# Moving the exponentials, coefficients, powers and K of heads 16 to 31 to later groups of a state-space and FFN kernel

## The chip, the cores and the metric

The kernel runs on one core of one Trainium2 chip. The metric is the device time of one execution in microseconds (us); lower is better. The kernel before takes 305.06 us, the median of three runs (304.72 to 305.21).

## The reference

The input x has 128 sequences (b), 32 heads (h) and 512 positions (l). Each head first gets a causal convolution with a kernel K that is made from 64 complex exponentials, plus a skip term; positions beyond a sequence's length are zeroed. Then comes a gated FFN over the 512 positions with 1376 inner features, its inputs rounded to fp8, and the result is added to x:

```
dt = exp(log_dt);  A = -exp(log_A_real) + 1j*A_imag;  dtA = A*dt
Ct = C * (exp(dtA) - 1) / A
K[h, l] = 2 * Re( sum_n Ct[h, n] * exp(dtA[h, n] * l) )
y = causal_conv(x, K) + x * D;   y[b, :, l >= length[b]] = 0
q = fp8(y)
hidden = silu(q @ gate.T) * (q @ up.T)
out = x + fp8(hidden) @ down.T
```

## The kernel before, in words

**Groups.** The 32 heads are worked in eight groups of four, numbered 0 to 7 (loop at line 764). A group has three stages. Gate and up (`gate_up`, line 630) runs over eleven chunks of 128 inner features: TensorE makes `gp` and `up` (line 646, four matmuls each), ScalarE takes silu of `gp` (L654), VectorE multiplies it with `up` (L656), and the product is rounded to fp8 by ScalarE (L621) and VectorE (L622, L623, L624) into `hq`. Then the convolution of the *next* group's four heads runs (`conv`, line 572): per head a matmul `sp` (L490) and five matmuls `cp` (L495 to L499) with a Toeplitz tile `st`; ScalarE copies `sp` to `shared` (L493); VectorE makes `q` and masks it (L576, L586); `sort` (line 589) permutes q by matmuls `pq` (L593), and ScalarE writes `qs` (L601), which the next group's gate and up reads. Between these stand the down matmuls `dp` (L688) of the present group, whose results VectorE adds to x (`put_out`, L701) before they are stored.

**K.** The heads fall into three batches for making K: heads 0 to 3, 4 to 15 and 16 to 31, in the objects `first`, `others[0]` and `others[1]` of class `Powers`. One batch takes these steps: `angles` (VectorE, L254, L52, L54, L264), `magnitudes` (ScalarE, one Exp per head, L269, then an activation at L198 that brings the Silu table back), `sines` (ScalarE, L276, L277, L281), `coefficients` (twelve small VectorE operations, L291 to L304), `products` (six VectorE operations, L309 to L324) and `response` (line 326). `response` makes K by one small matmul for each head into the PSUM tile `kp` and one more for the skip term (L329, L330), copies it to `kt` (VectorE, L333), and writes that to a DRAM buffer `kpad` (L334). `toeplitz` (line 470) reads each head's tile `st` back from `kpad` by two DMAs (L475, L476); there are four `st` buffers. Heads 16 to 19, the first that need batch `others[1]`, are group 4, and their convolution runs in the loop's iteration g = 3.

**Where batch `others[1]` is made before.** Its sixteen exponentials stand ahead of group 0, together with the twelve of `others[0]` (lines 713 to 716). Its angles are spread over the four `put_out` calls of iteration 0, its sines follow at that iteration's end (L827), coefficients and products are spread over the `put_out` calls of iteration 1, five at a time, and `response` is called after the gate and up of group 2 (line 769).

**Other ScalarE work.** `check_q` (line 603) sums the absolute values of q in two halves (L607). `low_halves` (line 535) sums the low halves of the weights (L542), four pieces in each iteration until nineteen are done.

**What sets the order.** Each engine runs its own instructions strictly in the order in which they stand; the build places them there, and `with after(x)` asks that an instruction stand behind x. Data dependencies are kept by semaphores on which an engine waits in place. SP's queue issues the `st`, `x` and `kpad` DMAs one behind the other; group 1's `st` loads and the second batch's `kpad` go through GpSimd's queue.

```
                if g == 2:
                    others[1].response()
...
                some = {0: (others[1].angles(), 2), 1: (itertools.chain(others[1].coefficients(), others[1].products()), 5)}
...
                with after(sent):
                    list(itertools.islice(lows, 4))
```

Of the kernel before, what the change touches and what calls it, by code (L numbers as in the profile page):

```python
# [15 lines left out]
AF = mybir.ActivationFunctionType  # L16
# [41 lines left out]
def ssm_fp8_ffn(  # L58
# [55 lines left out]
    def load_x(g, queue=nc.sync):  # L114
        xg = xp.tile([P, LC, T], F32, name="xg", bufs=1)
        queue.dma_start(
            xg.rearrange("p c (h b) -> p c h b", b=B),
            xT[:, g * HG : (g + 1) * HG, :].rearrange("(c p) h b -> p c h b", p=P),
        )
        return xg  # L120
# [13 lines left out]
    def load_gate_up(w, src, i0, i1, queue=nc.sync):  # L134
        return queue.dma_start(w[:, :, i0:i1], src[:, i0:i1].rearrange("(c p) i -> p c i", p=P))
# [24 lines left out]
    NK = NC + NB  # L160
# [35 lines left out]
    def table(func, ready):  # L196

        return nc.scalar.activation(spare, ready, func)  # L198

    def after(done):  # L200

        return tc.issue_after(done.ins)
# [35 lines left out]
    class Powers:  # L238
# [24 lines left out]
            for o, r in ((self.cos, self.sin), (self.zb[0:N], self.zb[0:N])):  # L263
                yield nc.vector.scalar_tensor_tensor(o, r, -1.0, r, ALU.mult, ALU.min)  # L264

        def magnitudes(self, then=True):
            self.mag = self.tile("mag", NK, shared=False)
            for h in range(self.h0, self.h1):
                done = nc.scalar.activation(  # L269
                    self.mag[:, h - self.h0, :], idx, AF.Exp, scale=wre[:, h : h + 1]  # L270
                )
            with after(done):
                return table(AF.Silu, self.mag[:, 0, 0:1]) if then else done

        def sines(self, between=lambda: None):
            nc.scalar.activation(self.sin, self.sin, AF.Sin)  # L276
# [63 lines left out]
    with after(exp_there), after(square_there):  # L340
        silu_there = first.magnitudes()
# [18 lines left out]
    done, copied, _ = first.response()  # L360
# [32 lines left out]
    shared = [const.tile([P, 2, P], F32, name=f"shared{n}") for n in range(HG)]  # L393
# [170 lines left out]
    def narrow():  # L564
        with ExitStack() as arm:
# [6 lines left out]
            def conv(g, q, j, xg, xs, before):  # L572

                st, loaded = toeplitz(stp, g * HG + j, nc.gpsimd if g == 1 else nc.sync)
                cp, t, convolved, copied = convolve(st, xg, xs, j, inv[:, 0:1], before)
                nc.vector.scalar_tensor_tensor(  # L576
                    q[:, j, :].rearrange("p (k c l) -> p k c l", k=2, c=2),
                    cp.rearrange("p (k c) l -> p k c l", k=2),
                    inv[:, 0:1],
                    t,  # L580
                    ALU.mult,
                    ALU.add,
                    saturate=False,
                )
                words = q.bitcast(I32)[:, j, :]
                made = nc.vector.tensor_tensor(words, words, mask.bitcast(I32), ALU.bitwise_and)  # L586
                return convolved, made, loaded, copied

            def sort(q, qs, j, before):

                pq = ps.tile([P, NQ], F32, name="pq", tag="up")
                for c in range(LC):
                    done = nc.tensor.matmul(  # L593
                        pq[:, OFF[c] : OFF[c] + CAPS[c]],
                        q[:, j, CHUNKS.index(c) * P : (CHUNKS.index(c) + 1) * P],
                        perm[:, 0 : CAPS[c]],
                        start=True,
                        stop=True,
                    )
                with after(before):  # L600
                    return done, nc.scalar.activation(qs[:, j, :], pq, AF.Copy, saturate=False)  # L601

            def check_q(g, q):

                for n in range(2):
                    junk = vp.tile([P, T], F32, name="s")
                    done = nc.scalar.activation(  # L607
                        junk.bitcast(BF16),
                        q[:, n * HG // 2 : (n + 1) * HG // 2, :].rearrange("p h l -> p (h l)"),
                        AF.Abs,  # L610
                        accum_out=fin[:, 2 * g + n : 2 * g + n + 1],
                    )
                return done
# [96 lines left out]
            others = [Powers(n) for n in range(1, len(batches))]  # L710
            with after(copied):
                list(others[0].angles())
            with after(first_sines):
                silu_there = others[0].magnitudes(False)
            with after(silu_there):
                silu_there = others[1].magnitudes()
            with after(silu_there):
                sines_there = others[0].sines()
            list(others[0].coefficients())
            xg, xs = x0, xs0  # L720
            q = yp.tile([P, HG, L], F8, name="q")
            qs = yp.tile([P, HG, NQ], F8, name="qs")
            for j in range(HG):
                convolved, made, loaded, sines_there = conv(0, q, j, xg, xs, sines_there)
                if j == 0:
                    with after(made):
                        list(others[0].products())
                else:
                    with after(convolved):
                        done, sines_there = sort(q, qs, j - 1, sines_there)  # L730
            with after(loaded):
                load_gate_up(uw, upT, 0, I1)
                load_gate_up(gw, gateT, I2, IH)
                load_gate_up(uw, upT, I1, IH)
                load_gate_up(gw, gateT, IH, I)
                loaded = load_gate_up(uw, upT, IH, I)
# [10 lines left out]
            lows = low_halves(vp)  # L747
# [15 lines left out]
            halves = [*whole[:-1], (HG - 1, 0, L // 2), (HG - 1, L // 2, L)]  # L763
            for g in range(G):
                hq, multiplied, done, jobs = gate_up(g, qs, first_loads if g == 0 else {})
                if g == 0:
                    xn_next, xs_next = loads
                xn = xn_next
                if g == 2:
                    others[1].response()  # L770
                if g == G - 1:
                    break
                some = {0: (others[1].angles(), 2), 1: (itertools.chain(others[1].coefficients(), others[1].products()), 5)}
                d = Down(g, hq, xn, whole, ["dp", "dp", "cp", "cp"], *some.get(g, ()))
                xg, xs = x_next, xs_next
                q_done, q = q, yp.tile([P, HG, L], F8, name="q")
                qs = yp.tile([P, HG, NQ], F8, name="qs")

                last, sent = multiplied, None
                for j in range(HG):
                    if j in (0, 2):
                        with after(done):
                            *_, done = jobs.pop(0)
                    with after(last), after(done):
                        last, done, loaded, sent = conv(g + 1, q, j, xg, xs, sent)
                    if j == 1:
                        for n in range(2):  # L790
                            with after(last):
                                last = d.multiply(n, 0, EARLY)
                    if j >= 2:
                        with after(last):
                            last, sent = sort(q, qs, j - 2, sent)
                with after(loaded):
                    if g + 2 < G:
                        x_next = load_x(g + 2)
                if g + 2 < G:
                    xs_next, summed = load_sums(g + 2)  # L800
                with after(summed):
                    xn_next = load_sorted(g + 1)
                with after(sent):
                    list(itertools.islice(lows, 4))
                for n in range(2):
                    with after(last):
                        last = d.multiply(n, EARLY, LATE)
                for n in range(2, HG):
                    with after(last):
                        last, sent = sort(q, qs, n, sent)  # L810
                with after(sent):
                    check_q(g, q_done)
                for job in jobs:
                    with after(done):
                        *_, done = job
                with after(last):
                    last = d.multiply(2, 0, LATE)
                for n in range(HG):
                    if (g, n) == (G - 2, HG - 1):
                        break  # L820
                    with after(last):
                        last = d.multiply(n, LATE if n < 3 else 0, IC)
                    with after(done):
                        done = d.put_out(n)
                if g == 0:
                    with after(sent):
                        others[1].sines()  # L827
# [9 lines left out]
            with after(done):  # L837
                done = before.put_out(HG - 1)
# [135 lines left out]
```

## Time and profile before

| what | value |
|---|---|
| median of three runs | 305.06 us (304.72 to 305.21) |
| the profiled execution's own time | 305.09 us |
| its span in the profile | 303.2 us |
| TensorE's mean granted clock | 0.986 |
| VectorE busy | 264.3 us (87%) |
| ScalarE busy | 181.0 us (60%) |
| GpSimd busy | 50.8 us (17%) |
| the 28 exponentials of L269 ahead of group 0, first start to last end | 10.38 to 16.82 us |
| first gate matmul of group 0 | 28.69 us |

The profile is one execution. PE is TensorE's matmuls and PEld its weight loads, DVE is VectorE, ACT ScalarE, POOL GpSimd, and SPq the queue of SyncE that issues DMAs. A row of the timeline gives the start, the time until the end of the last of the merged instructions, the engine, the line of the kernel, the operation with output and input tiles, and in brackets how long the engine had been idle just before and what released it. Each fp32 matmul appears twice in the counts (x2). The page's first part gives busy times by engine; its second cuts the span into 40 slices of 7.58 us, each digit a tenth of busy time.

### The profile page before, as it was taken

Reading aid. Unit: us, or ns where it says so; the run is one execution under the profiler, and the core shown is the slowest. Engines: PE = TensorE matmul, PEld = TensorE weight load, DVE = VectorE, ACT = ScalarE, POOL = GpSimd, SP = SyncE. Lnnn points to the kernel's source line nnn. Section 1 sums busy time; section 2 is a strip of 40 time slices with the busy share of each in tenths; the row PEclk is TensorE's granted clock in tenths of the full one; section 3 lists DMA queues with packets and bytes.
Section 4 is the critical chain, followed back from the end, with each engine's and each line's share of the span. In section 5 each row is a group of like instructions: output and inputs, shape, how many; then the busy total and the mean of one; then the engine's idle time right before and its main releaser. Section 6 shows DMA issues by size and latency. Waiting matters only on the chain.

```text
span 303.2 us, 4843 instructions
## 1 busy us (share of the span) xinstructions
PE 283.9 (94%) x1708; PEld 171.3 (57%) x1708; DVE 264.3 (87%) x466; ACT 181.0 (60%) x385; POOL 50.8 (17%) x104
## 2 busy tenths in 40 slices
PE   8889999997999999999999999999999999999850
PEld 3467567454774557645774567555774567455330
DVE  5875999989999999969997899969996999899960
ACT  4964783877729783658726782748533881579200
POOL 5771340210002100130002100310003200000030
PEclk9999999999999999999999999999999999999995
DMA  2599999981069602792059404890259430000052
GB/s 83 192 261 381 378 361 341 256 278 44 20 128 243 271 1 50 193 316 111 22 129 311 201 1 89 248 304 21 58 148 294 175 125 0 0 1 3 0 214 72
DMA packets 26039, 47.95 MB, mean 158 GB/s; under 512 B 2848, under 2 KB 15404, under 8 KB 24088
## 3 DMA queue, kind: packets, MB, share of 16 engines
q1 hardware_dynamic: 21784, 26.28, 28.9%
q0 software_dynamic: 4224, 21.29, 20.8%
q8 instruction: 15, 0.25, 0.3%
q14 instruction: 16, 0.13, 0.2%
HBM read 39.03 MB, written 8.54 MB: 157 GB/s over the span
## 4 chain that ended last, share of the span: by engine, by line
DVE 44%; PE 29%; issue 12%; ACT 8%; DMA 3%; SPq 1%; POOL 1%; POOLq 0%; ACTq 0%
PE dp L688 11%; DVE v L656 10%; DVE v L622 10%; DVE hq L623 9%; PE gp L646 5%; DVE q L576 5%; ACT s L654 5%; PE up L646 4%; DVE hq L624 4%; ACT m L621 2%; DMA st<-kpad 2%; PE cp L497 1%; PE cp L495 1%; PE cp L496 1%; DVE q L586 1%
## 5 line engine op out<-in xcount | busy, mean ns | idle before, releaser
L688 PE MATMUL dp<-dw,hq 128*128 128x512 bf16 (+1 forms) x363 | 84.6, 380 | 3.1 <-DVE hq L624 2.5
L654 ACT ACTIVATE s<-gp,psc 128x512 f32<-128x512 f32 x88 | 58.5, 680 | 30.7 <-PE gp L646 30.3
L646 PE MATMUL up<-qs,uw 128*128 128x512 fp8e4 (+1 forms) x352 | 70.3, 321 | 2.3 <-DVE v L656 1.8
L656 DVE SCALAR_TENSOR_TENSOR v<-up,psc,s 128x512 f32<-128x512 f32 x88 | 64.3, 745 | 7.7 <-ACT s L654 7.7
L646 PE MATMUL gp<-qs,gw 128*128 128x512 fp8e4 (+1 forms) x352 | 70.4, 321 | 0.6 <-ACT qs L601 0.6
L688 PEld LDWEIGHTS <-hq 128*128 128x128 bf16 x363 | 33.2, 96 | 44.5 <-DVE hq L624 7.5
L623 DVE SCALAR_TENSOR_TENSOR hq<-m,v 128x1024 bf16<-128x1024 bf16 (+1 forms) x56 | 55.5, 991 | 1.1
L622 DVE SCALAR_TENSOR_TENSOR v<-m,v 128x1024 f32<-128x1024 bf16 (+1 forms) x56 | 55.4, 989 | 1.2 <-ACT m L621 1.2
L621 ACT ACTIVATE m<-v 128x1024 bf16<-128x1024 f32 (+1 forms) x56 | 48.7, 870 | 8.9 <-DVE v L656 8.9
L646 PEld LDWEIGHTS <-uw 128*128 128x128 bf16 x352 | 32.0, 97 | 28.9 <-issue 3.8
L646 PEld LDWEIGHTS <-gw 128*128 128x128 bf16 x352 | 31.9, 97 | 26.4 <-issue 0.7
L601 ACT ACTIVATE qs<-pq 128x376 fp8e4<-128x376 f32 x32 | 14.6, 480 | 30.3 <-PE pq L593 30.3
L701 DVE SCALAR_TENSOR_TENSOR xn<-dp,nsc,xn 128x512 f32<-128x512 f32 (+1 forms) x33 | 23.0, 729 | 9.0 <-PE dp L688 8.8
L493 ACT ACTIVATE shared<-sp,inv 128x128 f32<-128x128 f32 x32 | 11.3, 360 | 27.6 <-PE sp L490 27.6
L576 DVE SCALAR_TENSOR_TENSOR q<-cp,inv,shared 128x512 fp8e4<-128x512 f32 x32 | 23.8, 744 | 2.1 <-PE cp L499 1.5
L111 POOL DMA_DIRECT2D xs<-xT x6 | 3.5, 586 | 116.4 <-PE sp L490 116.4
L706 POOL DMA_INDIRECT out<-xn,index x9 | 9.5, 1060 | 76.8 <-DVE xn L701 72.4
L624 DVE TENSOR_SCALAR hq<-hq 128x1024 bf16<-128x1024 bf16 (+1 forms) x56 | 20.9, 373 | 1.4
L495 PE MATMUL cp<-st,xg 128*128 128x256 f32 x64 | 19.2, 381 | 0.0
L497 PE MATMUL cp<-st,xg 128*128 128x256 f32 x64 | 19.1, 380 | 0.0
L496 PE MATMUL cp<-st,xg 128*128 128x256 f32 x64 | 19.0, 379 | 0.0
L607 ACT ACTIVATE s<-q 128x1024 bf16<-128x1024 fp8e4 x16 | 16.7, 1054 | 0.0
(159 smaller groups left out, 283.7 us busy)
## 6 DMA issues: line engine op xcount, KB each, us to landing
xg<-xT SPq DMA_DIRECT2D x8, 1024.0 KB, 7.7
st<-kpad SPq DMA_DIRECT2D x28, 192.0 KB, 3.8
st<-kpad SPq DMA_DIRECT2D x28, 128.0 KB, 3.5
xs<-xT POOLq DMA_DIRECT2D x12, 256.0 KB, 4.6
dw<-downT SPq DMA_DIRECT2D x2, 1280.0 KB, 19.3
gw<-gateT SPq DMA_DIRECT2D x2, 768.0 KB, 8.6
gw<-gateT SPq DMA_DIRECT2D x1, 1216.0 KB
uw<-upT SPq DMA_DIRECT2D x1, 1216.0 KB
```

The source lines that it names most:

```text
L495: nc.tensor.matmul(cp[:, 1:4:2, :], xg[:, 0, b], st[:, 2:4, :], start=True, stop=False)
L497: nc.tensor.matmul(cp[:, 1:3, :], xg[:, 1, b], st[:, 3:5, :], start=False, stop=False)
L576: nc.vector.scalar_tensor_tensor(q[:, j, :].rearrange("p (k c l) -> p k c l", k=2, c=2), cp.rearrange("p (k c) l -> p k c l", k=2), inv[:, ...
L621: nc.scalar.activation(m, v, AF.Abs, scale=2.0**20 * (1.0 + 2.0**-6), accum_out=acc)
L622: yield nc.vector.scalar_tensor_tensor(v, m, 1.5 * 2.0**14, v, ALU.max, ALU.add)
L623: yield nc.vector.scalar_tensor_tensor(out, m, 1.5 * 2.0**14, v, ALU.max, ALU.subtract)
L624: yield nc.vector.tensor_scalar(out, out, FP8_MAX, -FP8_MAX, ALU.min, ALU.max)
L646: multiplied = nc.tensor.matmul(o[:, :, 0 : CAPS[c]], w[:, c, i * P : (i + 1) * P], qs[:, :, OFF[c] : OFF[c] + CAPS[c]], start=(c == 0), s ...
L654: gated = nc.scalar.activation(s, gp, AF.Silu, scale=pgate)
L656: done = nc.vector.scalar_tensor_tensor(v[:, (i - i0) * T : (i - i0 + 1) * T], up, pup, s, ALU.mult, ALU.mult)
L688: done = nc.tensor.matmul(self.dps[n], self.hq[:, i, j * B : (j + 1) * B], dm[:, i, l0:l1], start=(i == 0), stop=(i == IC - 1),)
L701: added = nc.vector.scalar_tensor_tensor(o, self.dps[n], ndown, o, ALU.mult, ALU.add)
```

## The change

Five things are changed, all to do with batch `others[1]` (heads 16 to 31):

1. Its sixteen exponentials leave the stretch ahead of group 0 and stand in iteration 0, behind the ScalarE copy of the second sorted head; `magnitudes` always ends with the activation that brings the Silu table back. `mag` becomes a tile that both later batches share.
2. In iteration 0 they stand where four `low_halves` were; those of all later iterations move on by one iteration.
3. `check_q` of group 0 is split: its first half stands ahead of group 0 (behind the third head), its second in the convolution stage of iteration 0.
4. The coefficients stay in iteration 1 (three for each `put_out`), and the products move to iteration 2 (two for each `put_out`).
5. `response` is called after the gate and up of group 3 instead of group 2.

```diff
-        def magnitudes(self, then=True):
-            self.mag = self.tile("mag", NK, shared=False)
+        def magnitudes(self):
+            self.mag = self.tile("mag", NK)
...
-                return table(AF.Silu, self.mag[:, 0, 0:1]) if then else done
+                return table(AF.Silu, self.mag[:, 0, 0:1])
...
-                silu_there = others[0].magnitudes(False)
-            with after(silu_there):
-                silu_there = others[1].magnitudes()
+                silu_there = others[0].magnitudes()
...
+                    if j == 2:
+                        with after(sines_there):
+                            sines_there = check_q(0, q, (0,))
...
-                if g == 2:
+                if g == 3:
                     others[1].response()
...
-                some = {0: (others[1].angles(), 2), 1: (itertools.chain(others[1].coefficients(), others[1].products()), 5)}
+                some = {0: (others[1].angles(), 2), 1: (others[1].coefficients(), 3), 2: (others[1].products(), 2)}
...
+                        if g == 0:
+                            with after(sent):
+                                sent = check_q(0, q_done, (1,))
...
                 with after(sent):
-                    list(itertools.islice(lows, 4))
+                    if g == 0:
+                        sent = others[1].magnitudes()
+                    else:
+                        list(itertools.islice(lows, 4))
...
-                with after(sent):
-                    check_q(g, q_done)
+                if g:
+                    with after(sent):
+                        check_q(g, q_done)
```

In the built program the engines' orders differ as follows. On TensorE ahead of group 0, before: `sp`, `cp` of head 0, `sp`, `cp` of head 1, `sp` of head 2, `sp` of head 3, three `cp` of head 2, `pq` of head 0, and so on; after: `sp`, `cp`, `sp`, `cp`, `pq` of head 0, `sp`, `cp` of head 2, `pq` of head 1, `sp`, `cp` of head 3, `pq` of head 2. The 17 `kp` matmuls of the last batch stand before in four pieces (2, 7, 1 and 7) among group 2's last gate and up matmuls; after, in one piece behind the last `up` matmul of group 3 and directly ahead of the `sp` of head 16. The copy to `kt` stands behind the same L624 of VectorE in both, one group later. On SP's queue the write of `kpad` and the `st` loads of heads 16 to 19 follow it, behind the load of group 4's x. ScalarE has two more loads of a function table, around the sixteen exponentials.

More of the change, by code (lines that the diff above doesn't have):

```diff
@@ L601, in sort, with check_q @@
                     return done, nc.scalar.activation(qs[:, j, :], pq, AF.Copy, saturate=False)
-            def check_q(g, q):
-                for n in range(2):
+            def check_q(g, q, halves=(0, 1)):
+                for n in halves:
                     junk = vp.tile([P, T], F32, name="s")
```

## The prediction

> **What bounds the kernel now.** I read the page's slices first: TensorE is full nearly everywhere, and in most slices VectorE is as full.
>
> ```profile
> span 303.2 us, 4843 instructions
> PE 283.9 (94%) x1708; PEld 171.3 (57%) x1708; DVE 264.3 (87%) x466; ACT 181.0 (60%) x385; POOL 50.8 (17%) x104
> PE   8889999997999999999999999999999999999850
> DVE  5875999989999999969997899969996999899960
> ACT  4964783877729783658726782748533881579200
> ```
>
> Then busy times from one first gate matmul to the next, for groups 1, 2, 3 and 4 (us; busy PE, PEld, DVE, ACT, POOL; clock).
>
> ```profile
> 62.48:98.21 35.73, 33.74 (x197) 20.35 (x196) 33.57 (x60) 24.86 (x49) 4.27 (x4) 1.00 0.47 137
> 98.21:133.00 34.79, 34.79 (x232) 21.58 (x231) 32.48 (x53) 21.73 (x47) 3.56 (x4) 1.00 0.51 147
> 133.00:166.30 33.30, 33.09 (x198) 20.21 (x196) 29.84 (x44) 20.62 (x45) 3.56 (x4) 1.00 0.51 163
> 166.30:199.60 33.30, 33.09 (x198) 20.22 (x197) 29.83 (x44) 20.02 (x43) 3.58 (x4) 1.00 0.50 143
> ```
>
> A plain group takes 33.30 us with TensorE busy for 33.09: TensorE's in-order stream is the bound, and VectorE (29.84) follows closely. So only what removes or adds time in that stream moves the end. Three places differ from plain: the stretch ahead of group 0 (28.69 us), group 1 (+2.43) and group 2 (+1.49). The timeline tells why. Ahead of group 0:
>
> ```profile
> 10.38 6.44 ACT L269 ACTIVATE mag<-idx,wre 128x49 f32<-128x49 f32 x28
> 16.84 1.28 ACT L198 ACT_TABLE_LOAD   x1
> ...
> 20.73 0.39 PE L499 MATMUL cp<-st,xg 128*128 128x128 f32 x2
> 20.96 0.39 PE L490 MATMUL sp<-st,xs 128*128 128x128 f32 x2
> 22.08 0.46 PE L490 MATMUL sp<-st,xs 128*128 128x128 f32 x2 [0.74 <-DMA st<-kpad]
> ```
>
> TensorE stands still from 21.12 to 22.08, because head 3's `sp` is queued ahead of head 2's `cp` and its tile `st` lands at 21.95. And where K of the last batch is made and read back:
>
> ```profile
> 114.16 0.23 PE L330 MATMUL kp<-sm,last 1*32 1x16 f32 x2
> 114.32 0.49 PE L490 MATMUL sp<-st,xs 128*128 128x128 f32 x2
> 115.35 0.67 DVE L333 COPY kt<-kp 32x512 f32<-32x512 f32 x1
> 116.09 0.33 SPq L334 DMA_DIRECT2D kpad<-kt  x1
> 118.43 0.33 SPq L475 DMA_DIRECT2D st<-kpad  x1
> ```
>
> The `sp` at 114.32 is not of this batch: it convolves group 3, whose `st` had long landed. The road from copy to `kpad` to `st` is covered by a whole group of other work.
>
> **Part 1, ahead of group 0: -0.95 us.** An exponential costs 6.44 / 28 = 0.23 us, so without sixteen the twelve end at 13.14, the table load and L198 near 14.65. The sines gain less: they need VectorE's angles, which end at 17.28. They start there instead of 18.25, and head 0's q near 19.2 instead of 20.02. That alone moves nothing, since TensorE runs until 21.12 without waiting. What moves is its order: `pq` of head 0 and both matmul sets of head 2 now come before head 3's `sp`, so the stop of 22.08 - 21.12 = 0.96 us goes. I replayed the queues: head 1's q is masked by 22.9 (the products go ahead of it) and its `pq` comes at 23.2; head 3's `sp` at 23.4 finds `st` landed; the last `pq` comes near 26.8 instead of 27.78. The first half of `check_q` (1.05 us, plus 0.2 to read the sum) falls at 22.9 to 24.1 on ScalarE, ahead of head 3's `shared`, needed at 25.4: hidden by `cp` of head 3; uncovered it costs up to 1.25. Group 0 starts at 27.7. Ends: -1.2, and -0.3 if group 1's `st` or the down weights, which land at 41 to 50 us in slices full of DMA, do not come earlier with it.
>
> **Part 2, exponentials in iteration 0: 0.** They stand behind the `qs` copy that ends at 54.53, and ahead of the last two `qs`: 1.28 + 16 x 0.23 + 1.28 + 0.2 = 6.44 us, to 60.97; the two `qs` take 0.73 more (59.87 to 60.60 before), to 61.7. Group 1's first gate matmul comes at 62.48, behind down matmuls. So 0.78 us of slack remain, where the four L542 (5.44 us) left 1.9. [...] In this trace the load at 16.84 begins 0.02 us after the exponentials and L198 follows 0.02 us after it[...]. By the row the part is free[...]. I take the row. The second half of `check_q` lies in ScalarE's wait for `sp` (3.21 us ahead of 49.92); the L542 that move on stand beside down matmuls as before, 5.44 us of them already did so in iteration 1. Both 0. Angles and sines, to which I put group 1's +2.43, stay where they are.
>
> **Part 3, coefficients and products: 0.** All eighteen VectorE operations together (some 4.4 us) lie at 95.7 to 102.7, and TensorE's matmuls follow each other at 0.64 us from 98.21 to 105.28 without a gap. What cost nothing there can't be won back; spread out it costs nothing either. Ends -0.2 and +0.2.
>
> **Part 4, `kp` leaves group 2: -1.5 us.** From the first `up` to the next group's `sp`, group 2 takes 114.32 - 98.85 = 15.47 us, group 3 147.37 - 133.63 = 13.74. The four gaps that the `kp` pieces make sum to 2.0 us and explain it. From that `sp` on group 2 is 0.25 us quicker than group 3, so its excess is 1.49, all of it back.
>
> **Part 5, `kp` behind group 3: +8.3 us.** Here the change adds a wait. I put it on the clock of before:
> - The last `up` is over at 147.37, where the next `sp` starts. Then come the 17 `kp`: the second batch's 12 took 0.87 us and its L330 0.16 (26.64 to 27.67), so 16 take 1.16 + 0.16 = 1.32, to 148.7.
> - VectorE reaches L333 behind L656 and L624, which end near 149.5. The copy takes 0.67, to 150.19. SP issues `kpad` 0.07 later, 150.26.
> - From that issue to the first `st` issue it was 118.43 - 116.09 = 2.34: 152.60.
> - An `st` load lands after 3.1 us (median, stretch 149 to 160) to 3.6 (116 to 128); I take 3.3: 155.9, and `sp` starts at 156.0.
>
> `sp` of head 16 is 8.65 us late, with TensorE still for 7.3 of them. Queued behind it are all of group 4's convolution and group 3's down matmuls, and nothing can pass. The other three heads' loads are issued at about 0.95 us each and the matmuls need 2.0 us a head, so they add nothing. VectorE meanwhile finishes 2.9 us of rounding and then waits for `cp` too; being ahead later, it spares the 0.3 us that the 26 down matmuls at 160.11 lose (6.19 us instead of 26 x 0.226). Net 8.3. Ends: 7.0 (`kpad` back in 1.43 us as for the first batch, `st` in 3.0) and 9.8 (`st` in 4.8).
>
> **Part 6, TensorE's clock after the stop: +1.7 us.** Before, TensorE never stands still for as long. Its only cold stretch is the start:
>
> ```profile
> 1.34 4.93 PE L233 MATMUL nothing<-still 128*128 128x512 bf16 x14 [1.34 <-POOL still L173]
> ...
> 6.37 2.76 PE L233 MATMUL nothing<-still 128*128 128x512 bf16 x12
> ```
>
> Fourteen matmuls at the later pace would take 14 x 2.76 / 12 = 3.22 us; they took 4.93. The loss is 1.7 us. [...] By the rows between 6 and 290 us nothing would be lost, as they hold no such stop[...]. I take the start's row, 1.7[...].
>
> **Sum.** Against the profiled execution's own 305.09 us (span 303.2 and 1.89 around it): -0.95 - 1.5 + 8.3 + 1.7 = +7.55, so 312.6. The median of the runs is 305.06, no different.
>
> **Rivals.**
> - *The clock stays up* through the stop: 310.9. For it: the granted clock is 1.00 in every group. Against it: the matmuls at the start are slow though that row says full. Chance 0.20.
> - *A longer road*: [...]`st` at 4.8 us[...]. 313.6 to 316.5. For it: `st` loads took 8.1 us (median) in the stretch 45 to 55, full of other transfers; against it: DMA is quiet around 150. Chance 0.20.
> - *Faster*: the road kpad to `st` hides. It would have to be shorter than VectorE's lead: `sp` could start right behind `kp` only if `st` were there at 148.7, 7.3 us earlier than worked out. Then -0.95 - 1.5 + 1.3 - 0.3 = -1.45 gives 303.6. It decides from a stop under 1.4 us. For it: nothing in the order of the queues, since `kp`, copy, `kpad`, `st` and `sp` each need the one before. Chance 0.03.
> - *Nothing to be seen* (the gains and a stop of 1.4 us cancel): 0.01.
>
> The forecast itself has 0.56. A measurement of this kernel can tell about 0.2% (0.6 us) from no change. Faster 0.03, same 0.01, slower 0.96. The range 310.2 to 315.2 takes in the clock that stays up and the nearer half of the longer road.
>
> **What would show it.** In the profile after: first gate matmul of group 0 at about 27.7; group 1's first about 34 us later with no wait for `qs`; group 2 at 33.3 us; L333 about 2 us behind the last `up` of group 3; the first `st` of head 16 issued 2.3 us behind `kpad`; an idle TensorE of about 7 us before one `sp`, named as waiting for `st`; and `cp` matmuls of the first heads behind it at twice their 0.22 us each. I am wrong if `st` lands before TensorE reaches it, or if another group grows.

## The result and the profile after

The changed kernel takes 313.12 us (median of four runs, 312.57 to 313.73). The kernel before takes 305.13 us in the runs beside it. The ratio is 1.026, with a 95% interval of 1.024 to 1.028: slower by 8.0 us. The profiled execution took 312.57 us.

First comes the page of the changed kernel, its head and two rows of its 40 slices (7.77 us each).

```profile
span 310.6 us, 4826 instructions
...
PE   8899999989999999997399999999999999999860
...
PEclk9999999999999999999789999999999999999995
```

TensorE's row has one new hole, in slices 18 and 19 (counted from 0), from 140 to 155 us. The row of the granted clock dips beside it, in slices 19 and 20. Before, that row read 9 in every slice but the last.

The next view cuts the span at each group's first gate matmul: groups 2, 3 and 4 of the changed kernel. The columns are the length, the busy times of PE, PEld, DVE, ACT and POOL, then the clock.

```profile
96.81:130.11 33.30, 32.96 (x195) 20.22 (x196) 31.26 (x50) 23.59 (x46) 3.87 (x4) 1.00 0.39 127
130.11:173.97 43.86, 36.78 (x229) 23.37 (x230) 31.99 (x49) 21.49 (x47) 3.56 (x4) 0.92 0.46 135
173.97:207.27 33.30, 32.96 (x195) 20.22 (x196) 29.84 (x44) 20.62 (x45) 3.88 (x4) 1.00 0.52 153
```

Group 2 has come down to the plain 33.30 us, from 34.79. Group 3 has gone from 33.30 to 43.86. Groups 4 to 6 keep their lengths. The timeline of the changed kernel shows what lies inside group 3.

```profile
144.58 1.20 PE L329 MATMUL kp<-ang,ga 128*32 128x32 f32 x32
...
146.59 0.67 DVE L333 COPY kt<-kp 32x512 f32<-32x512 f32 x1
...
147.33 0.33 SPq L334 DMA_DIRECT2D kpad<-kt  x1
...
149.63 0.34 SPq L475 DMA_DIRECT2D st<-kpad  x1
...
152.81 0.77 PE L490 MATMUL sp<-st,xs 128*128 128x128 f32 x2 [6.87 <-DMA st<-kpad]
...
153.37 1.06 PE L495 MATMUL cp<-st,xg 128*128 128x256 f32 x2
...
156.78 0.63 PE L490 MATMUL sp<-st,xs 128*128 128x128 f32 x2
...
157.86 0.59 PE L496 MATMUL cp<-st,xg 128*128 128x256 f32 x2
```

The road runs downwards: matmuls, copy, write, first read, `sp`. TensorE stands still for 6.87 us and the row names `st` as what ended it. Nothing passed `sp`: the down matmuls queued behind it read `hq`, which VectorE last wrote at 150.12 (the end of an L624), and still start only at 159.40. Head 16's three wide `cp` rows (L495 to L497) then take 1.06 us each, where the row at 157.86 takes 0.59. Head 16 lasts 3.97 us, from 152.81 to 156.78. At full pace a head lasts 2.01.

Cutting the same stretch finely gives the clock.

```profile
149.50:150.50 1.00, 0.00 (x0) 0.00 (x0) 0.59 (x2) 0.00 (x0) 0.00 (x0) 1.00 0.00 0
150.50:151.50 1.00, 0.00 (x0) 0.00 (x0) 0.00 (x0) 0.00 (x0) 0.00 (x0) 0.66 0.49 124
...
152.81:157.20 4.39, 4.39 (x14) 3.85 (x15) 0.10 (x1) 0.37 (x1) 0.00 (x0) 0.50 0.84 212
157.20:158.00 0.80, 0.80 (x4) 0.68 (x4) 0.77 (x2) 0.37 (x1) 0.00 (x0) 0.72 0.05 6
```

The clock falls to half about 4.9 us after the last `kp` matmul has ended (145.93): 0.66 over one microsecond is half rate from about 150.8. It is back at about 157.65, as 0.72 over 0.80 us is half rate for 0.45. So 4.84 us of work (152.81 to 157.65) ran at half rate, and half of that, 2.4 us, is the loss. The two heads say the same: (3.97 - 2.01) + (2.39 - 1.96) = 2.39.

| where | before, us | after, us | difference |
|---|---|---|---|
| first `sp` of group 0 | 16.95 | 16.45 | -0.50 |
| from there to group 0's first gate matmul | 11.74 | 10.77 | -0.97 |
| group 0 | 33.79 | 33.93 | +0.14 |
| group 1 | 35.73 | 35.66 | -0.07 |
| group 2 | 34.79 | 33.30 | -1.49 |
| group 3 | 33.30 | 43.86 | +10.56 |
| all the rest | | | -0.19 |
| profiled execution | 305.09 | 312.57 | +7.48 |

The first row is no edit's: the first `sp` lay between 16.4 and 17.8 us in the profiles of this study, whatever the kernel. Without it the sum is +7.98, and the medians differ by 7.99. The size of the second row also depends on the execution, as the experiments on the stretch ahead of group 0 show.

### The profile page after: what moved, and what is told of

It is laid out like the page before. It is cut to its first block, busy times and chain, and to the rows that moved or that the text cites. A ratio compares the mean times of both kernels' runs of the same rounds, so it can differ in the third digit from the quotient of the medians.

```text
span 310.6 us, 4826 instructions
## 1 busy us (share of the span) xinstructions
PE 284.6 (92%) x1692; PEld 173.1 (56%) x1708; DVE 265.3 (85%) x466; ACT 183.9 (59%) x388; POOL 51.9 (17%) x104
## 4 chain that ended last, share of the span: by engine, by line
DVE 39%; PE 29%; issue 11%; DMA 8%; ACT 8%; POOL 1%; POOLq 0%; SPq 0%; ACTq 0%
PE dp L688 13%; DVE v L656 11%; DVE v L622 9%; DVE hq L623 8%; DMA dw<-downT 7%; ACT s L654 5%; DVE q L576 4%; DVE hq L624 3%; PE gp L646 2%; ACT m L621 2%; PE cp L495 2%; PE cp L497 2%; PE cp L496 2%; PE up L646 2%; PE nothing L233 2%
## 5 line engine op out<-in xcount | busy, mean ns | idle before, releaser
L688 PE MATMUL dp<-dw,hq 128*128 128x512 bf16 (+1 forms) x348 | 81.4, 380 | 4.1 <-DVE hq L624 2.1
L624 DVE TENSOR_SCALAR hq<-hq 128x1024 bf16<-128x1024 bf16 (+1 forms) x56 | 20.9, 373 | 1.4
L490 PE MATMUL sp<-st,xs 128*128 128x128 f32 x64 | 13.9, 302 | 6.9 <-DMA st<-kpad 6.9
L495 PE MATMUL cp<-st,xg 128*128 128x256 f32 x64 | 19.8, 393 | 0.0
L497 PE MATMUL cp<-st,xg 128*128 128x256 f32 x64 | 19.5, 387 | 0.0
L496 PE MATMUL cp<-st,xg 128*128 128x256 f32 x64 | 19.5, 387 | 0.0
```

The source lines that it names most:

```text
L495: nc.tensor.matmul(cp[:, 1:4:2, :], xg[:, 0, b], st[:, 2:4, :], start=True, stop=False)
L496: nc.tensor.matmul(cp[:, 0:4:2, :], xg[:, 2, b], st[:, 2:4, :], start=False, stop=False)
L497: nc.tensor.matmul(cp[:, 1:3, :], xg[:, 1, b], st[:, 3:5, :], start=False, stop=False)
L624: yield nc.vector.tensor_scalar(out, out, FP8_MAX, -FP8_MAX, ALU.min, ALU.max)
L688: done = nc.tensor.matmul(self.dps[n], self.hq[:, i, j * B : (j + 1) * B], dm[:, i, l0:l1], start=(i == 0), stop=(i == IC - 1),)
```

## The experiments

The theory is the prediction's own: `sp` of head 16 waits for the road from `kp` through `kpad` to `st`, TensorE then runs at half rate for a while, and nothing else of the change costs anything. What else could have taken the time (the spread of the small steps, the clock not at all, or the group rather than the place in it) stands as a rival with each run. The kernel before took 305.07 to 305.18 us beside all of these; each median is of four to 22 runs. No kernel here leaves work out; the second adds some, matmuls whose output nothing reads.

| kernel | median, us | ratio to before, 95% |
|---|---|---|
| before, only K moved to behind group 3 | 314.2 | 1.027 to 1.031 |
| after, the stop filled with matmuls | 309.34 | 1.011 to 1.015 |
| after, coefficients, products and K as before | 304.34 | 0.997 to 0.999 |
| after, K early in group 3 | 303.99 | 0.994 to 0.998 |
| after, K behind the eighth chunk of group 3 | 309.02 | 1.006 to 1.015 |
| before, TensorE's new order only | 305.95 | 1.001 to 1.003 |
| before, TensorE's and VectorE's new order | 305.06 | 0.999 to 1.001 |
| after, TensorE's old order for head 3's `sp` | 313.75 | 1.024 to 1.030 |
| after, K early in group 3, angles and sines later | 303.43 | 0.993 to 0.997 |
| the same, sines later still | 302.29 | 0.988 to 0.991 |

**Is it K alone?** The kernel before, with one line changed.

```diff
-                if g == 2:
+                if g == 3:
                     others[1].response()
```

> The kernel before with one edit: K of heads 16 to 31 is made behind group 3's gate and up instead of group 2's; exponentials, coefficients, products and the order ahead of group 0 stay. Theory (the exposed road kp, kt, kpad, st to head 16's sp plus half-rate matmuls behind the stop is the whole loss): group 2 gets 1.5 us shorter, group 3 about 10.5 us longer, sum +9.0, so 314.1 us, longer than the changed kernel by the 1.4 us that it gained ahead of group 0. Rival (the exponentials behind the gate, with two more table loads and a mag tile that two batches share, are part of the loss): below 312.6 us.

Measured: 314.2 us, +9.0 on before, as the theory has it. Group 3 takes 44.09 us, with a stop of 6.8 us ahead of `sp` and head 16 again at 3.97 us. Group 2 took 33.96 us and not the plain 33.30. The five products for each `put_out` lie there at the start of group 2, whose gate and up stage took 0.66 us longer than a plain one (15.04 against 14.38). VectorE's products stand between its first steps of that stage, and TensorE then waits for VectorE. The timeline of this kernel:

```profile
105.76 0.80 PE L646 MATMUL up<-qs,uw 128*128 128x512 fp8e4 x4 [0.15 <-DVE v L656]
```

In the kernel before, group 2 held the same products and `kp` and was 1.49 us above plain; `kp` in the middle of another group costs 1.39 (K in group 3, but early, below). Added up they would be 2.05, so in the kernel before the products' cost lay under that of `kp`.

**How much of it is the clock?** The stop of the changed kernel filled with matmuls on a constant tile.

```diff
...
-                    others[1].response()
+                    made_k, *_ = others[1].response()
+                    with after(made_k):
+                        multiplied = keep_busy(26)
```

> The changed kernel with 26 matmuls on a tile of zeros between the last kp and head 16's sp; they feed nothing. Theory (the cp behind the stop are slow because TensorE's clock has fallen): the 26 take some 5.8 us of the 6.9 us stop, the clock row stays at 1.0, head 16's five cp take 1.7 us again instead of 3.4, and 2.3 to 2.4 us come back: 310.7 us. Rival (they are slow because they wait for their st tiles): no change, 313.1 us. If the fillers outlast the stop, they would add up to 1 us.

The timeline of this kernel:

```profile
146.13 5.78 PE L233 MATMUL nothing<-still 128*128 128x512 bf16 x25
153.07 0.46 PE L491 MATMUL sp<-st,xs 128*128 128x128 f32 x2 [1.16 <-DMA st<-kpad]
153.37 0.60 PE L496 MATMUL cp<-st,xg 128*128 128x256 f32 x2
```

`sp` begins where it did, since the road is as long, but `cp` takes 0.60 us from the first and head 16 lasts 2.04; the granted clock reads 1.00 over the whole group. Group 3 takes 41.50 us, 2.36 less than in the changed kernel. That is the price of the clock, and the other 8.2 us are the road, with about 0.1 for the products that now stand at the group's start. (The trace records 25 of the 26 added matmuls.) The median fell by more, 3.8 us. In this execution 0.8 us of it lies behind the last group, where the closing wait of the queue was shorter than in the changed kernel (its longest piece 1.1 us, not 2.1). No edit explains that, and it stays open.

**K back in group 2.** The exponentials and `check_q` as changed, the rest as before.

```diff
-                if g == 3:
+                if g == 2:
...
-                some = {0: (others[1].angles(), 2), 1: (others[1].coefficients(), 3), 2: (others[1].products(), 2)}
+                some = {0: (others[1].angles(), 2), 1: (itertools.chain(others[1].coefficients(), others[1].products()), 5)}
```

> The changed kernel with coefficients, products and K where they were before (group 1 and group 2); only the exponentials and the sums of q are moved. Theory: the gain ahead of group 0 alone is left, -1.4 us less a wait of 0.1 for the down weights: 303.8 us. Rival (the exponentials in iteration 0 make group 1 late, their slack being 0.2 us): 304.5 us or more.

Measured 304.34 us, -0.8: nearer to the rival's bound of 304.5 than to 303.8, though below it. In its profile first `sp` to first gate is 10.76 us, the changed kernel's own figure, so the gain ahead of group 0 is there. A part of it is gone by the end: group 0 is 0.16 us longer than before, with a down matmul that waits 0.41 us for its weights, and group 2 is 0.18 us longer. Group 1's first gate matmul, which the rival expected late, starts right behind the down matmuls. So the time comes near the rival's, but not for its reason.

**K in group 3, but early.** `response` behind the second chunk of group 3's gate and up.

```diff
+            def response_2(hq):
+                others[1].response()
+
+            hooks = {0: {8: sorted_0, 9: sums_1}, 3: {1: response_2}}
...
-                if g == 3:
-                    others[1].response()
...
```

> The changed kernel, but the last batch's kp matmuls stand behind the second chunk of group 3's gate and up instead of behind the eleventh; copy, kpad and st follow from there. Theory: the road of some 8 us lies beside nine more chunks (12.5 us), no stop and no half rate; left are the gain ahead of group 0 (-1.4), group 2 (-1.5) and the kp themselves (+1.4 to +2.0), so 303.6 to 304.1 us against 305.1. Rival (something else of the change costs too, such as products that now delay the start of group 3): 305 us or more.

It holds: 303.99 us. Group 3 takes 34.69 us, the plain 33.30 and 1.39 for `kp`, at a clock of 1.00. The road is under nine chunks of gate and up: `kpad` is issued at 135.1 us, and head 16's `sp` starts at 146.0 without a wait. So group 3 itself isn't the fault: the place within it is.

**K behind the eighth chunk.** The same with `3: {7: response_2}`, three chunks ahead of the end.

> The changed kernel with K's matmuls behind the eighth chunk of group 3's gate and up. Theory: the road of 6.9 us behind kp outlasts the three chunks left by 2.7 us, so TensorE stops for 2.7 us; [...]the cp behind it keep their pace, and the time is that of K behind the second chunk plus 2.7 us: 306.7 us. Rival (any such stop brings half rate): 2.4 us more, 309.1 us.

The timeline of this kernel:

```profile
149.57 0.46 PE L490 MATMUL sp<-st,xs 128*128 128x128 f32 x2 [3.41 <-DMA st<-kpad]
149.87 0.97 PE L495 MATMUL cp<-st,xg 128*128 128x256 f32 x2
150.64 1.06 PE L496 MATMUL cp<-st,xg 128*128 128x256 f32 x2
```

The stop is halved, but the clock falls all the same (to 0.50), and only after TensorE has resumed: `sp` is at full pace (0.46 us), the `cp` behind it at half (1.06 us, not 0.59). The stop was also longer than the theory had it, 3.41 us and not 2.7. That a stop of 2.7 us leaves the pace alone was the author's estimate, and this run doesn't show it either way. The four runs were 308.69, 309.75, 309.35 and 306.94 us. Three lie near the rival (309.1), one near the theory (306.7). The mean granted clock was 0.984, 0.979, 0.984 and 0.989; with K behind the second chunk, where the clock of group 3 stays at 1.00, it was 0.987 to 0.991. So the clock probably stayed up in the fourth run. The profile shows half rate in the first; by their times and mean clocks the second and third probably had it too. Why the fourth did not is not shown.

**The stretch ahead of group 0.** Three kernels take apart what gained 0.97 us there. First, the kernel before with TensorE's order as changed and all 28 exponentials still ahead.

```diff
-                convolved, made, loaded, sines_there = conv(0, q, j, xg, xs, sines_there)
+                with after(done) if j >= 2 else ExitStack():
+                    convolved, made, loaded, sines_there = conv(0, q, j, xg, xs, sines_there)
```

> The kernel before with TensorE's order ahead of group 0 as in the changed kernel (head 2's cp and the first pq ahead of head 3's sp), all 28 exponentials still ahead of group 0. Theory (the gain is the removed wait for head 3's st, not the shorter ScalarE work): group 0 starts 0.95 us earlier, 304.1 us. Rival (the exponentials hold ScalarE, so shared and qs come late and the earlier order only meets another wait): 305.1 us; a mixture: between.

Measured: 305.95 us, the median of 22 runs. The theory fell. The profiled execution, 304.99 us, is the fastest of the 22; it has 12.06 us from `sp` to the gate where before has 11.74, but does not show what makes the others slower. Its timeline has another stop:

```profile
21.79 0.34 PE L593 MATMUL pq<-perm,q 128*128 128x128 bf16 x4 [1.12 <-DVE q L586]
```

`pq` waits for head 0's mask, which stands on VectorE behind head 1's q, and that waits for head 1's `cp`. So VectorE's order was changed too:

```diff
-                with after(done) if j >= 2 else ExitStack():
+                with after(done) if j >= 2 else ExitStack(), after(made) if j == 1 else ExitStack():
```

> The kernel before with both TensorE's and VectorE's order ahead of group 0 as in the changed kernel (also head 0's mask and the products ahead of head 1's q), all 28 exponentials still ahead of group 0. Theory now (the gain is the order on two engines; the earlier exponentials only brought the scheduler to it): from the first sp to group 0's first gate 10.8 to 11.0 us instead of 11.7, 304.3 to 304.5 us. Rival (with the late sines head 0's mask comes too late for the earlier pq, as in the order of TensorE alone, 12.1 us): 305.2 us or more.

The timeline of this kernel:

```profile
21.18 0.34 PE L593 MATMUL pq<-perm,q 128*128 128x128 bf16 x4 [0.34 <-DVE q L586]
```

305.06 us and 11.68 us: the median shows no gain. The stop is shorter, but head 0's mask is still late, since the sines are. Last, the converse: the changed kernel with head 3's `sp` put back ahead of head 2's `cp`.

```diff
...
+            def start_last(xs):
+                early["st"] = toeplitz(stp, HG - 1)
+                early["sp"], done = start_shared(early["st"][0], xs, HG - 1)
+                return done
...
+                    early["sp"] if (g, j) == (0, HG - 1) else None,
+                    (lambda: start_last(xs)) if (g, j) == (0, 2) else None,
...
```

> The changed kernel with head 3's sums back ahead of head 2's candidates in TensorE's order (as in the kernel before); the twelve early exponentials and all else stay as changed. Theory (the gain ahead of the first gate needs both the earlier sines and the new order, since the old order puts the wait for head 3's stream ahead of work that is ready): from the first sums of the angles to the first gate matmul 11.3 to 11.8 us where the changed kernel has 10.77, with TensorE stopped 0.5 to 1.1 us ahead of head 3's sums; median 313.6 to 314.1 where the changed kernel has 313.1. Rival (the earlier sines alone suffice): 10.8 us, no such stop, 313.1.

Measured: 11.26 us, just short of what the theory asked, and 313.75 us. The median falls in the theory's range, but 0.36 us of this execution's excess over the changed kernel lies in group 3 (44.22 us). The stop is only 0.27 us, and the row names another reason than expected:

```profile
21.43 0.46 PE L489 MATMUL sp<-st,xs 128*128 128x128 f32 x2 [0.27 <-ACT qs L619]
```

So neither theory holds whole. How finely can this stretch be measured? The first experiment (K alone) left the code ahead of group 0 as before, yet its execution takes 11.30 us there and not 11.74. Its first `sp` came 0.60 us later (17.55, not 16.95), but head 3's `sp`, which waits for `st`, only 0.16 later (22.24, not 22.08):

```profile
22.24 0.46 PE L490 MATMUL sp<-st,xs 128*128 128x128 f32 x2 [0.30 <-DMA st<-kpad]
```

So the same code differs by 0.44 us between two executions. The changed order with early sines is steadier: 10.76 to 10.85 us in seven executions, whose first `sp` lay between 16.44 and 17.81 us. As far as two executions of the old code tell, the gain ahead of group 0 is therefore 0.5 to 1.0 us, and 0.97 is the upper end. What each part adds to the other shows in these executions: with early sines the old order costs 0.49 us (11.26 against 10.77, the first `sp` at 16.52 and 16.45), and with the new order the late sines cost 0.91 (11.68 against 10.77, at 16.68 and 16.45). What either gives alone is not shown, since 11.26 and 11.68 lie within or beside the 11.30 to 11.74 of the unchanged code.

**A better place for each step.** Group 1's excess of 2.4 us had been put down to angles and sines. Here K comes behind the fourth chunk of group 3, the angles one for each `put_out` over iterations 0 and 1, the sines at the end of iteration 1, and coefficients and products in iteration 2.

```diff
...
+            hooks = {0: {8: sorted_0, 9: sums_1}, 3: {3: response_2}}
+            angles = others[1].angles()
...
-                some = {0: (others[1].angles(), 2), 1: (others[1].coefficients(), 3), 2: (others[1].products(), 2)}
+                some = {0: (angles, 1), 1: (angles, 1), 2: (itertools.chain(others[1].coefficients(), others[1].products()), 5)}
...
-                if g == 0:
+                if g == 1:
...
```

> The changed kernel with K early in group 3 (behind the fourth chunk), the angles of heads 16 to 31 one operation at each put_out of iterations 0 and 1, the sines at the end of iteration 1, coefficients and products in iteration 2. Theory: group 1's extra 2.4 us come from VectorE's angles (3.9 us at one place) delaying its first v; spread, most of that goes, while the sines (1.7 us of ScalarE) now fall at the start of group 2: 302.0 to 303.0 us. Rival (the sines are what holds group 1 up): the extra time only moves to group 2, 303.8 us.

Measured 303.43 us, half a microsecond short: group 1 fell by 1.37 us to 34.30, but group 2 rose by 1.07 to 34.37, its ScalarE now holding sines beside `low_halves` and gate and up. Two of the six angle operations and all the sines left the start of group 1 together, so the 1.37 is not split between them. Group 1 is still 1.0 us above plain; the other four operations still stand around its start, but whether they are the reason was not tested. So the sines went into the down stage of iteration 2, where four `low_halves` had been:

```diff
...
+                    elif g == 2:
+                        sent = others[1].sines()
...
-                if g == 0:
-                    with after(sent):
-                        others[1].sines()
```

> As the kernel with spread angles, but the sines stand in iteration 2 in place of that iteration's four sums of low halves (which move on), where ScalarE has room, instead of at the start of group 2. Theory: group 2 loses the 1.1 us that the sines cost it: 302.4 us. Rival (coefficients and products, not the sines, delay group 2): 303.4 us.

It holds: 302.29 us (301.99 to 302.57), 2.9 below before and the fastest of all. Groups 2 and 3 of this kernel:

```profile
95.65:128.94 33.29, 33.09 (x197) 20.22 (x196) 30.95 (x55) 20.33 (x42) 3.86 (x4) 1.00 0.37 114
128.94:163.50 34.56, 34.43 (x231) 21.42 (x230) 32.50 (x53) 23.28 (x44) 3.65 (x4) 1.00 0.62 176
```

Group 2 is plain; group 3 holds `kp` (34 more matmul instructions) at the cost of their own time and no more.

## Why the prediction was right, point by point

- **The whole.** Forecast 312.6 us, measured 313.12, by the likeliest course: `sp` late for the road through `kpad`, then half rate. Without the first row of the table above the profile's change is +7.98 where +7.55 was forecast: Part 6 gave 0.7 us more, Part 5 0.2 less, all else together less than 0.1. So the match is no cancelling of large errors.
- **Part 1, -0.95: -0.97, with some luck, for a reason told half right.** The prediction said that the earlier sines move nothing and the order does it all. The runs show that 10.77 us needs both: without the early sines 0.91 us is lost, without the new order 0.49. The match to 0.02 is luck: against the other execution with the old code ahead of group 0 (11.30 us), the gain is 0.5. The stop was also read as 0.96 us; the row names 0.74 us of idle time. (The `sp` ahead of it starts at 20.96 and a following matmul could start about 0.22 later, so the time lost is 0.9.)
- **Part 2, 0: right.** In the timeline of the changed kernel:

```profile
53.66 1.28 ACT L269 ACT_TABLE_LOAD   x1
...
54.95 3.73 ACT L269 ACTIVATE mag<-idx,wre 128x49 f32<-128x49 f32 x16
...
58.70 1.28 ACT L198 ACT_TABLE_LOAD   x1
...
60.00 0.20 ACT L198 ACTIVATE spare<-mag 128x1 f32<-128x1 f32 x1
```

The whole took 6.54 us (53.66 to 60.20), where 6.44 was worked out. The first exponential starts 0.01 us behind its load, the second load 0.02 us behind the last exponential, and L198 0.02 us behind that load: each load took 1.28 us here and nothing more. The cover was nearly used up: `qs` ends at 60.95 and the gate matmul starts at 61.15, without a wait. The slack left is 0.2 us, not 0.78. Group 0's +0.14 is another thing: a `dp` matmul at 46.34 waits 0.41 us for the down weights, which the prediction named as the low end of Part 1.
- **Part 3, 0 (-0.2 to +0.2): right in sum.** The spread products cost 0.09 us at the start of group 3, whose gate and up takes 14.47 us against 14.38. But "what cost nothing there can't be won back" did not hold as a rule: with `kp` gone, five products for each `put_out` cost 0.66 us in the first experiment. A cost can lie under a larger one.
- **Part 4, -1.5: -1.49.**
- **Part 5, +8.3: +8.1.** The road's pieces, forecast and measured: `kp` 1.32 and 1.35; `kpad` to first `st` issue 2.34 and 2.30; issue to `sp` 3.4 and 3.18; stop 7.3 and 6.87. Beyond the 0.09 of Part 3, `sp` is 8.23 us later in its group than a plain group's. VectorE's lead spared 0.16 us of that (14.80 from 159.17 to 173.97, 14.96 before) where 0.3 was forecast.
- **Part 6, +1.7: +2.4.** This is the term that was mis-sized. The kernel's slow start was the only row at hand and gave 1.7; filling the stop gave back 2.36. That a stop inside the kernel slows TensorE by as much as the start was the author's estimate: the kernel before holds no such stop (TensorE's longest wait there is 1.4 us). What the sum needed was half of the time that work ran slow, 4.84 / 2 = 2.42. The start's row has 3.4 us of it (from 1.33 to 4.72 us its weight loads begin 0.43 us apart, where the later matmuls take 2.76 / 12 = 0.23) and so half of that, 1.7; this stop left more behind. Other executions left 3.4 to 5.5 us (last section).

The rivals: the clock did not stay up, the road was not longer, and nothing hid it. How far the longer road could reach (316.5) was the author's estimate. Of the signs against itself the prediction named two. `st` did not land before TensorE reached it, but a group other than group 3 did grow: group 0 by 0.14 us, for the wait for the down weights told above.

## What to carry to other kernels

When a value goes from one engine through DRAM to another, add up the road (here 0.7 us from the end of `kp` to the copy, 0.7 for the copy, 2.3 to the first read, 3.2 to the matmul: 6.9 us), and put its start at least that far ahead of its first reader in the in-order stream. The same step cost nothing but its own 1.3 to 1.4 us in the same group, seven to nine chunks earlier. Price a stop of the matmul engine at its length plus half of the slow time after it (2.4 us here, 1.7 to 2.7 in the four profiles with a stop of 3.4 to 7.0 us), and look under a cost before calling the smaller one beside it free (0.66 us beside 1.39 here).

## What the runs showed of the hardware that was not expected

- The clock's fall came at no fixed time after the stop's start: 4.9 us after TensorE's last matmul in the changed kernel (a stop of 6.87 us), 3.8 in the one with K behind the eighth chunk (3.41 us), and 2.05 in the one with the old order, whose stop was as long as the changed kernel's (7.03 us). With K behind the eighth chunk the half rate therefore hit the work after the stop, and none of the stop. The old order's clock around its stop, then that of K behind the eighth chunk:

```profile
147.40:148.40 1.00, 0.00 (x0) 0.00 (x0) 1.00 (x2) 0.11 (x2) 0.00 (x0) 1.00 0.00 0
148.40:149.40 1.00, 0.00 (x0) 0.00 (x0) 0.97 (x2) 0.00 (x0) 0.00 (x0) 0.50 0.48 70
...
158.00:158.70 0.70, 0.70 (x3) 0.52 (x3) 0.67 (x2) 0.37 (x1) 0.00 (x0) 0.55 0.08 29
```

```profile
149.57:150.50 0.93, 0.93 (x4) 0.84 (x5) 0.90 (x2) 0.37 (x1) 0.00 (x0) 0.70 1.00 143
...
152.50:153.50 1.00, 1.00 (x7) 1.00 (x6) 0.00 (x0) 0.00 (x0) 0.00 (x0) 0.57 0.53 163
```

- The price of a stop varied too. Work ran at half rate for 4.84 us in the changed kernel, 5.25 with the old order (153.38 to 158.63), some 5.46 with K alone moved (154.96 to about 160.42, since its `cp` at 160.21 takes 0.70 us, between the 1.06 before it and the 0.59 after) and 3.4 behind the eighth chunk (149.94 to 153.36). Half of each is the loss: 2.4, 2.6, 2.7 and 1.7 us.
- The granted clock reads 0.50 in the stop's wake, but 1.00 at the start of the kernel before (1.34 to 6.20 us), although fourteen matmuls took 4.93 us there and twelve of the same 2.76 right after. The first of them ran at about half pace (weight loads 0.43 us apart), so that row shows the falls inside these kernels but not the slow start. That the clock is what slowed the start is likely, not shown.
